# Sliding-window attention with one packed block of weights: the scores of the block behind go where the mask would be

## The chip, the cores and the metric

The kernel runs on one core of a Trainium2 chip, as one launch. The metric is the device time of that launch in microseconds. Engines in the text: PE is TensorE, DVE is VectorE, ACT is ScalarE, POOL is GpSimd, SP is SyncE, which here only issues DMAs.

## What is computed

The input is x of 2 sequences, 4096 tokens, 256 channels, in fp32. First a recurrent block (a token mix, three projections, a scan over time, a group norm and an output projection) is added to a layer norm of x. Then, after another layer norm, two layers follow, each with local attention and a gated feed-forward part, and a residual around all. The attention is what matters here:

```
WINDOW = 128, HEADS = 8, DIM_HEAD = 64, DEPTH = 2
bq = q.reshape(b, h, w, WINDOW, d) * 8
bk, bv = look_around(k), look_around(v)      # the block behind, and the own block: 256 keys
sim = einsum('bhwid,bhwjd->bhwij', bq, bk)
mask = (i < j) | (i > j + WINDOW) | (j == -1)
attn = softmax(where(mask, -max, sim))
out = einsum('bhwij,bhwjd->bhwid', attn, bv)
```

So query i of a block sees the keys i to 127 of the block behind, and the keys 0 to i of its own: 129 keys of the 256, whatever i is. The first block of a sequence has none behind it and sees only its own.

## The kernel before

The work is noted down in program order by functions that each issue a few operations (`project`, `scores`, `softmax`, `transpose_p`, `values`, `output` and so on). A planner (`Plan`) takes them all, with the dependences it finds from overlapping regions of tiles, and simulates five engines and eight PSUM banks with a table of costs (`cost`). At every step it gives an engine the operation that can start first, ties going to the smaller row (about the window's number). That order is then written out, and is fixed on the chip: each engine and the SP queue go through their own list, and an operation at the head of a list that waits holds all behind it. Operations noted with `either` (copies out of PSUM, and the products `scaled`) go to VectorE or ScalarE, whichever the planner has free first. Matmuls noted within one `piece` stay together. Since the planner emits all operations from one function, most rows of the profile have one line, L497, and are told apart by their tiles. `scaled` is L491 on DVE and L493 on ACT.

The planner charges a DMA 2000 ns and 512 bytes for every element of its largest operand's free size at 170 bytes a nanosecond, whatever the number of partitions, and lets such transfers follow one another.

There are 128 windows of attention: two sequences, two layers, 32 blocks of 128 tokens. Window n is worked on in one turn of a loop, while the projections of n+1 and the output and feed-forward of earlier ones are done. The recurrence of the first sequence runs ahead of all windows; that of the second runs beside the first 54 windows.

In one window:

- `project(n, j)` makes q, k and v, 128x512 each. v goes to a tile `vt` (three buffers). q and k are rotated on POOL and DVE, and `transpose_qk` turns them into `qT` and into one of the two slots of `kT`, by the parity of n.
- `scores(n)` is one piece: first `values(n - 1)`, then eight score products of 256 keys. They fill four banks (`sims`), each for two heads.
- `softmax(n, g)` takes bank g: for each of two heads one fused operation on DVE reads the bank, negates it, adds the mask, writes the tile `pr` in SBUF, and takes the minimum; ACT makes the exponential in place with its sum; a reciprocal; and `scaled` normalises. A bank is free once the fused operations have read it.
- `transpose_p(n, g)` turns the weights of two heads on TensorE, 128x128 at a time (four transposes into one bank), and copies them out as `pT`, 128x512.
- `values(n)` multiplies: for each head, `vt` of the window behind by its part of `pT`, and `vt` of the own window by the other part, both into one bank. It waits for the four `pT` of the window.

A window without one behind it does half of that. Four are of that kind.

Of the kernel before, what the change touches and what calls it, by code (L numbers as in the profile page):

```python
# [10 lines left out]
AF = mybir.ActivationFunctionType  # L11
ALU = mybir.AluOpType
AX = mybir.AxisListType
PSUM = bass.MemoryType.PSUM

P = 128
B, S, D = 2, 4096, 256
HD_A = 16
L, HEADS, DH, W = 2, 8, 64, 128
INNER = HEADS * DH  # L20
# [5 lines left out]
T = 512  # L26
NW = T // P
NB = S // T
# [4 lines left out]
MASKED = -3e38  # L33
# [12 lines left out]
)  # L46
WNOW = 3 * (2 * T + 2)
RA = 10764
PRS, PTS = 6, 4

# [22 lines left out]
class View:  # L75
# [51 lines left out]
    def to_broadcast(self, shape):  # L127
        return View(
            self.place,
            self.rows,  # L130
            np.broadcast_to(self.idx, shape[1:]),
            [*self.chain, ("to_broadcast", (shape,), {})],
        )

    def mask(self):
        n = self.place.size
# [34 lines left out]
class Plan:  # L171
# [35 lines left out]
    def bank(self, shape):  # L207

        return self.view(Place(T, True), 0, shape)
# [9 lines left out]
    @contextmanager  # L219
    def piece(self):  # L220

        self.open = []
        yield
        self.open = None
# [276 lines left out]
def kernel(ctx: ExitStack, tc: tile.TileContext, a: dict, out: bass.AP):  # L501
# [6 lines left out]
    tile_of, bank, piece = plan.tile, plan.bank, plan.piece  # L508
    act, dve, either = nc.scalar.copy, nc.vector.tensor_copy, nc.either.copy
# [4 lines left out]
    ident, gmat = (mats[:, i, :] for i in range(2))  # L514
# [286 lines left out]

    mask = tile_of([P, 3 * W], "mask")
    lnp = tile_of([P, L, 2, 2], "lnp")
    b1 = tile_of([P, L, 2, NM], "b1")
    qks = tile_of([P, L, 4 * DH], "qks")

    def later_loads():
        nc.sync.dma_start(out=wot, in_=a["w_ot"])  # L810
        nc.sync.dma_start(out=mask[:, : 2 * W], in_=a["c_mask"])
        nc.sync.dma_start(out=mask[:, 2 * W :], in_=a["c_mask"][:, :W])
        nc.sync.dma_start(out=lnp, in_=a["p_ln"])
        nc.sync.dma_start(out=b1, in_=a["p_b1"])
        nc.sync.dma_start(out=qks, in_=a["p_qk"].partition_broadcast(P))
# [16 lines left out]
            nc.sync.dma_start(out=w2, in_=a["w_2"][l])  # L832


    kT = tile_of([P, HEADS // 2, 2, W], "kT")


    hm = tile_of([P, NM, T], "hm")
# [4 lines left out]
    G_LAST = 5  # L843
    blocks = [(l, b, c) for b in range(B) for l in range(L) for c in range(NB)]
    xs, xTs, hs, x1s, zs, hTs, rems = ({} for _ in range(7))
    tabs, qks_of, vts, qTs, pos, sims, prs, sqs, t2s = ({} for _ in range(9))


    def load(k):
# [73 lines left out]
    def project(n, j):  # L923
        k, w = divmod(n, NW)
        xT = xTs[k]

        hT = (xT[:, 0, 1 + w * P : 1 + (w + 1) * P], xT[:, 1, w * P : (w + 1) * P])
        pm = bank([P, INNER])
        for i in range(2):
            nc.tensor.matmul(  # L930
                pm, hT[i], wqkv[:, i, j * INNER : (j + 1) * INNER], start=(i == 0), stop=(i == 1)
            )
        if j == 2:
            vts[n] = tile_of([P, INNER], "vt", 3)
            either(vts[n], pm)
            return
        if j == 0:
            qks_of[n] = tile_of([P, 2, HEADS, DH], "qk", 2)
        either(qks_of[n][:, j].rearrange("p h d -> p (h d)"), pm)

    def square(n):
        qk = qks_of[n]
# [42 lines left out]
    def transpose_qk(n):  # L985
        qk = qks_of.pop(n)
        qT = qTs[n] = tile_of([P, HEADS // 2, P], "qT", 2)
        for j, dst in ((1, kT[:, :, n % 2, :]), (0, qT)):
            pt = bank([P, HEADS // 2, P])
            for hp in range(HEADS // 2):  # L990
                nc.tensor.transpose(
                    pt[:, hp, :],
                    qk[:, j, 2 * hp : 2 * hp + 2, :].rearrange("p h d -> p (h d)"),
                    ident,
                )
            either(dst, pt)

    def seen(n):

        me = n % 2  # L1000
        if n % (NB * NW) == 0:
            return slice(me, me + 1), mask[:, W : 2 * W], ((me, n),)
        if me:
            return slice(0, 2), mask[:, : 2 * W], ((0, n - 1), (1, n))
        return slice(0, 2), mask[:, W:], ((0, n), (1, n - 1))

    def scores(n):


        cs, _, _ = seen(n)  # L1010
        qT = qTs[n]
        sims[n] = [bank([P, 2, 2, W]) for _ in range(4)]
        with piece():
            if n:
                values(n - 1)
            for hp in range(HEADS // 2):
                for r in range(2):
                    s, m = divmod(hp, 2)
                    nc.tensor.matmul(
                        sims[n][2 * s + r][:, m, cs, :].rearrange("p c j -> p (c j)"),  # L1020
                        qT[r * DH : (r + 1) * DH, hp, :],
                        kT[r * DH : (r + 1) * DH, hp, cs, :].rearrange("p c j -> p (c j)"),
                        start=True,
                        stop=True,
                    )

    def softmax(n, g):

        cs, msk, _ = seen(n)
        sim = sims[n][g]  # L1030
        pr = prs[n, g] = tile_of([P, 2, 2, W], "pr", PRS)
        nmx = tile_of([P, 2], "nmx", 8)
        sums = tile_of([P, 2], "sums", 8)
        for m in range(2):
            ph = pr[:, m, cs, :].rearrange("p c j -> p (c j)")

            nc.vector.tensor_tensor_reduce(
                ph,
                sim[:, m, cs, :].rearrange("p c j -> p (c j)"),
                msk,  # L1040
                -1.0,
                3.0e38,
                ALU.add,
                ALU.min,
                nmx[:, m : m + 1],
            )
            nc.scalar.activation(
                ph, ph, AF.Exp, bias=nmx[:, m : m + 1], scale=-1.0, accum_out=sums[:, m : m + 1]
            )
        nc.vector.reciprocal(sums, sums)  # L1050
        for m in range(2):
            ph = pr[:, m, cs, :].rearrange("p c j -> p (c j)")
            nc.either.scaled(ph, ph, sums[:, m : m + 1])

    def transpose_p(n, g):

        cs, _, srcs = seen(n)
        pr = prs.pop((n, g))
        ppt = bank([P, 2, 2, W])
        for m in range(2):  # L1060
            for c, _ in srcs:
                nc.tensor.transpose(ppt[:, m, c, :], pr[:, m, c, :], ident)
        pT = prs[n, g, "T"] = tile_of([P, 2, 2, W], "pT", PTS)
        either(pT[:, :, cs, :], ppt[:, :, cs, :])

    def values(n):

        _, _, srcs = seen(n)
        po = bank([P, HEADS // 2, P])
        pTs = [prs.pop((n, g, "T")) for g in range(4)]  # L1070
        for hp in range(HEADS // 2):
            s, m = divmod(hp, 2)
            for i, (c, src) in enumerate(srcs):
                for r in range(2):
                    h = 2 * hp + r
                    nc.tensor.matmul(
                        po[r * DH : (r + 1) * DH, hp, :],
                        vts[src][:, h * DH : (h + 1) * DH],
                        pTs[2 * s + r][:, m, c, :],
                        start=(i == 0),  # L1080
                        stop=(i == len(srcs) - 1),
                    )
        pos[n] = po

# [202 lines left out]
    for j in range(3):  # L1287
        project(0, j)
# [6 lines left out]
    for n in range(NN + 6):  # L1295
        k, w = divmod(n, NW)
        here, ahead, behind = n < NN, n + 1 < NN, 0 < n <= NN
        plan.at(n)
        if here:
            transpose_qk(n)  # L1300
# [22 lines left out]
            rotate(n + 1, 0)  # L1323
        if here:
            scores(n)
        elif n == NN:
            with piece():
                values(n - 1)
# [23 lines left out]
        fill(n, 0)  # L1352
        if here:
            transpose_p(n, 0)
            transpose_p(n, 1)
        if ahead:
            project(n + 1, 2)
            cosines(n + 1)
        fill(n, 1)
        if here:  # L1360
            transpose_p(n, 2)
            transpose_p(n, 3)
        if ahead:
            rotated(n + 1)
        fill(n, 2)
# [7 lines left out]
def _constants():  # L1373

    f = np.float32
    p = np.arange(P)
    mats = np.zeros((P, 2, P), f)
    mats[:, 0, :] = np.eye(P)
    mats[:, 1, :] = (p[:, None] // HD_A == p[None, :] // HD_A) / f(HD_A)
    j = np.arange(2 * W)  # L1380
    mask = np.where((j[None, :] >= p[:, None]) & (j[None, :] <= p[:, None] + W), f(0), f(MASKED))

    half = np.arange(0, DH, 2, dtype=f)
    inv = f(1) / np.power(f(10000.0), half / f(DH))
    t = np.arange(S, dtype=f)
    freqs = t[:, None] * inv[None, :]
    base = (half + f(0.4 * DH)) / f(1.4 * DH)
    power = (t - f(S // 2)) / f(W // 2)
    scale = np.power(base[None, :], power[:, None])
    cos, sin = np.cos(freqs), np.sin(freqs)  # L1390
    rot = np.empty((S, 2, 2, DH), f)
    for q, sc in ((0, scale * f(8)), (1, f(1) / scale)):
        rot[:, 0, q, :] = np.concatenate([cos * sc, cos * sc], -1)
        rot[:, 1, q, :] = np.concatenate([-sin * sc, sin * sc], -1)
    rot = rot.reshape(NB * NW, P, 4 * DH)
    return {"c_mats": mats, "c_mask": mask.astype(f), "c_rot": np.ascontiguousarray(rot)}
# [52 lines left out]
```

## Time and profile before

| | |
|---|---|
| median of 3 runs | 3110.5 us (3108.18 to 3110.82) |
| the profiled execution, its own time | 3112.78 us |
| its span, first to last instruction | 3110.8 us |
| granted TensorE clock, mean | 0.995 |
| PE, DVE, ACT, POOL busy | 98%, 82%, 60%, 43% |
| transposes of attention weights | 2016, 270.5 us busy |
| mean rate of the DMA engines | 42 GB/s |

A row of the profile's groups reads: line, engine, operation, output<-inputs, shapes, count | busy us, mean ns of one | us of idle time of that engine just before them, and what ended it. The busy time of a group of matmuls includes the tail of the last one, since they are pipelined; the distance from one start to the next is what an instruction takes from the engine. In the timeline a row is: start, duration, engine, operation, and in brackets how long the engine had been idle and what released it.

### The profile page before, as it was taken

What the parts mean: (1) busy time and instruction counts of PE and PEld (TensorE: products, weight loads), DVE (VectorE), ACT (ScalarE), POOL (GpSimd) and SP (SyncE); (2) the same over time, 40 slices, a digit from 0 to 9 for tenths busy, and PEclk for the clock granted to TensorE, in tenths of its full rate; (3) what the DMA queues carried; (4) which work ended last, traced back from release to release, by engine and by line L of the source; (5) the groups of instructions that cost most, each with busy time, mean ns of one, the idle gap of its engine ahead of it and who ended that gap; (6) DMA issues with size and microseconds to landing.
All of it is one profiled execution on the core that took longest, in us unless ns stands there. A gap on an engine that the chain in (4) does not pass through costs nothing.

```text
span 3110.8 us, 47943 instructions
## 1 busy us (share of the span) xinstructions
PE 3061.6 (98%) x16368; PEld 2030.8 (65%) x16368; DVE 2539.1 (82%) x6306; ACT 1865.0 (60%) x4401; POOL 1339.6 (43%) x1581
## 2 busy tenths in 40 slices
PE   8979999999999999999999999999999999999998
PEld 3456666666666666666666666666666666666665
DVE  7889988888888888887787878787877777877774
ACT  6877866666666766665554555554555555555552
POOL 2227534443444444444444444443433444444440
PEclk9989999999999999999999999999999999999999
DMA  3222001110111210111112110111101110111000
GB/s 101 80 75 70 31 30 45 45 38 30 43 48 45 67 31 26 34 37 31 35 47 73 50 46 26 38 41 38 35 25 54 45 36 30 33 33 33 28 22 19
DMA packets 114837, 131.82 MB, mean 42 GB/s; under 512 B 13344, under 2 KB 100128, under 8 KB 114080
## 3 DMA queue, kind: packets, MB, share of 16 engines
q1 hardware_dynamic: 114592, 128.75, 13.2%
q8 instruction: 129, 2.11, 0.3%
q14 instruction: 116, 0.95, 0.1%
HBM read 78.38 MB, written 33.55 MB: 36 GB/s over the span
## 4 chain that ended last, share of the span: by engine, by line
PE 80%; DVE 10%; ACT 4%; POOL 2%; issue 2%; DMA 2%; SPq 0%; POOLq 0%; DVEq 0%; ACTq 0%
PE bank L497 80%; DVE arena L497 3%; ACT arena L497 1%; DMA h<-x 1%; DVE pr L497 1%; DVE sq L497 1%; DVE qk L497 1%; POOL rs L497 1%; ACT L497 1%; DVE hm L497 1%; POOL rn L497 1%; DVE x L497 1%; ACT qk L497 0%; SPq L497 0%; DVE pT L497 0%
## 5 line engine op out<-in xcount | busy, mean ns | idle before, releaser
L497 ACT ACTIVATE pr<-pr,nmx 128x256 f32<-128x256 f32 (+1 forms) x1024 | 504.2, 493 | 388.8 <-DVE nmx L497 388.4
L497 PE MATMUL bank<-wqkv,xT 128*128 128x512 f32 x1536 | 731.6, 599 | 0.0
L497 POOL TENSOR_TENSOR t<-qk,tab 128x256 f32<-128x256 f32 x512 | 387.6, 777 | 727.9 <-DVE qk L497 420.3
L497 PE MATMUL bank<-hT,w 128*128 128x512 f32 (+1 forms) x1408 | 645.9, 594 | 0.0
L497 PEld LDWEIGHTS bank<-hT,w 128*128 128x128 f32 (+1 forms) x1408 | 253.7, 189 | 251.9 <-issue 242.1
L497 PEld LDWEIGHTS bank<-wqkv,xT 128*128 128x128 f32 x1536 | 264.7, 190 | 229.9 <-issue 224.9
L497 DVE CUSTOM_DVE_ANT_0 pr<-bank,mask 128x256 f32<-128x256 f32 (+1 forms) x1024 | 372.5, 413 | 36.1 <-PE bank L497 36.0
L497 POOL TENSOR_TENSOR rn<-rn,mhalf 128x16 f32<-128x16 f32 x128 | 380.9, 2976 | 10.3
L497 PE MATMUL bank<-w,hm 128*128 128x256 f32 x1536 | 352.1, 379 | 0.0
L497 PEld LDWEIGHTS bank<-w,hm 128*128 128x128 f32 x1536 | 289.2, 190 | 57.7 <-issue 21.9
L497 PEld LDWEIGHTS bank<-mats,pr 128*128 128x128 f32 x2016 | 237.1, 141 | 114.2 <-issue 78.8
L493 ACT ACTIVATE pr<-pr,sums 128x256 f32<-128x256 f32 (+1 forms) x610 | 284.7, 495 | 35.1 <-DVE sums L497 33.4
L497 PEld LDWEIGHTS bank<-pT,vt 128*64 128x64 f32 x4032 | 217.5, 137 | 95.9 <-issue 88.3
L497 PE MATMUL bank<-mats,pr 128*128 128x128 f32 x2016 | 270.5, 273 | 2.3 <-DVE pr L491 1.2
L497 PE MATMUL bank<-kT,qT 64*128 64x256 f32 (+1 forms) x2048 | 253.4, 386 | 4.1 <-DVE nmx L497 4.1
L497 PE MATMUL bank<-pT,vt 128*64 128x128 f32 x4032 | 248.4, 276 | 0.0
L497 PE MATMUL bank<-wo,oT 128*128 128x256 f32 x1024 | 244.8, 382 | 2.2 <-ACT oT L497 1.2
L497 PEld LDWEIGHTS bank<-wo,oT 128*128 128x128 f32 x1024 | 192.2, 190 | 79.0 <-issue 38.3
L497 ACT COPY pT<-bank 128x512 f32<-128x512 f32 (+1 forms) x275 | 150.1, 572 | 120.0 <-PE bank L497 119.4
L497 PEld LDWEIGHTS bank<-kT,qT 64*128 64x128 f32 x2048 | 184.9, 186 | 44.6 <-issue 19.8
L497 POOL TENSOR_SCALAR rs<-mv 128x1 f32<-128x1 f32 x192 | 98.4, 517 | 248.4 <-DVE mv L497 242.2
L497 PE MATMUL bank<-arena,wold 128*128 128x256 f32 (+1 forms) x600 | 193.1, 447 | 0.0
(139 smaller groups left out, 4988.1 us busy)
## 6 DMA issues: line engine op xcount, KB each, us to landing
tab<-in_c_rot_dram SPq DMA_DIRECT2D x128, 128.0 KB
z<-zd SPq DMA_DIRECT2D x16, 512.0 KB
x<-in_x_dram SPq DMA_DIRECT2D x16, 512.0 KB
x1d<-x SPq DMA_DIRECT2D x16, 512.0 KB
x<-x1d SPq DMA_DIRECT2D x16, 512.0 KB
h<-x SPq DMA_DIRECT2D x128, 64.0 KB
xmd<-x SPq DMA_DIRECT2D x64, 128.0 KB
x<-xmd SPq DMA_DIRECT2D x16, 512.0 KB
```

Source lines behind the costliest of these rows:

```text
L493: self.nc.scalar.activation(dst, src, AF.Copy, scale=scale)
L497: getattr(getattr(self.nc, o.eng), name)(*args, **kw)
```

## The change

The 256 scores of a query are packed to 129. Where the causal mask would strike out a score of the own block (key j after query i), the score of key j-1 of the block behind is put in, which is one that the query sees. The oldest distance, key 127 of the block behind, is seen by all queries, and keeps a column of its own in front. The layout of a score bank becomes "behind, then own" for all windows, so `kT` gets a third slot; every second window a DMA copies the last slot to the first.

- On DVE, a predicated copy in PSUM (with the mask `packs`) puts the scores over the masked ones, and a reduction takes the minimum of the 129. The minus sign moves into the rotation table. ACT's exponential reads the bank itself and writes the 129 weights to `pr`, now one tile for eight heads, two buffers.
- `transpose_p` is called twice, with four heads of one block of 128 columns each. The turned weights are copied out as `pT`, and DVE also multiplies them by the mask `backs`, which keeps only those that belong to the block behind: `pB`. In the second call the first columns of the eight heads are turned together (128x8), copied to `last`, and a DMA puts them into row 0 of `pB`.
- `values` multiplies `pT` by the own values, and `pB` by `dv`, the difference between the value behind and the own value in whose place its weight sits. `differences(n)` makes `dv`: two DMAs shift the values behind by one row, POOL subtracts, and a DMA puts the value of key 127 in row 0.
- `vt` has two buffers for three, `pT` two for four, `pB`, `vr` and `dv` one.

```diff
-PRS, PTS = 6, 4
+PRS, PTS, PBS = 2, 2, 1
...
-        nc.sync.dma_start(out=mask[:, : 2 * W], in_=a["c_mask"])
-        nc.sync.dma_start(out=mask[:, 2 * W :], in_=a["c_mask"][:, :W])
+        for i, t in enumerate((packs, backs, later)):
+            nc.sync.dma_start(out=t, in_=a["c_mask"][:, i, :])
...
-    kT = tile_of([P, HEADS // 2, 2, W], "kT")
+    kT = tile_of([P, HEADS // 2, 3, W], "kT")
...
-            vts[n] = tile_of([P, INNER], "vt", 3)
+        vts[n] = tile_of([P, INNER], "vt", 2)
...
+    def differences(n):
+        if lone(n):
+            return
+        old, v = vts[n - 1], vts[n]
+        vr = tile_of([P, INNER], "vr")
+        dv = dvs[n] = tile_of([P, INNER], "dv")
+        nc.sync.dma_start(out=vr[1:P, :], in_=old[: P - 1, :])
+        nc.sync.dma_start(out=vr[0:1, :], in_=old[P - 1 : P, :])
+        nc.gpsimd.tensor_tensor(dv, vr, v, ALU.subtract)
+        nc.sync.dma_start(out=dv[0:1, :], in_=old[P - 1 : P, :])
...
+        if me == 2:
+            nc.sync.dma_start(out=kT[:, :, 0, :], in_=kT[:, :, 2, :])
...
     def softmax(n, g):
...
-            nc.vector.tensor_tensor_reduce(ph, sim..., msk, -1.0, 3.0e38, ALU.add, ALU.min, nmx[:, m : m + 1])
-            nc.scalar.activation(
-                ph, ph, AF.Exp, bias=nmx[:, m : m + 1], scale=-1.0, accum_out=sums[:, m : m + 1]
-            )
+            nc.vector.copy_predicated(
+                sim[:, :, W + 1 :],
+                packs[:, : W - 1].bitcast(mybir.dt.int32).unsqueeze(1).to_broadcast([P, 2, W - 1]),
+                sim[:, :, : W - 1],
+            )
+            nc.vector.tensor_reduce(nmx, sim[:, :, W - 1 :], AX.X, ALU.min)
...
+            nc.scalar.activation(
+                prs[n][:, h0 + 2 * m, off:], sim[:, m, W - 1 + off :], AF.Exp,
+                bias=nmx[:, m : m + 1], scale=-1.0, accum_out=sums[:, m : m + 1],
+            )
...
-    def transpose_p(n, g):
+    def transpose_p(n, s):
...
+        for h in range(4):
+            nc.tensor.transpose(ppt[:, h, :], pr[:, 4 * s + h, 1:], ident)
+        pT = pTs[n, s] = tile_of([P, 4, W], "pT", PTS)
+        either(pT, ppt)
...
+        nc.vector.tensor_tensor(
+            pBs[n][:, 4 * s : 4 * s + 4, :], ppt, backs.unsqueeze(1).to_broadcast([P, 4, W]), ALU.mult,
+        )
+        if s:
+            pt = bank([P, W])
+            nc.tensor.transpose(pt[:HEADS, :], pr[:, :, 0], ident)
+            last = tile_of([P, W], "last", 2)[:HEADS]
+            either(last, pt[:HEADS, :])
+            nc.sync.dma_start(out=pBs[n][0:1], in_=last)
...
     def values(n):
...
+                    w = (dvs if i else vts)[n]
+                    p = pBs[n][:, h, :] if i else own[h // 4][:, h % 4, :]
...
             scores(n)
+            differences(n)
...
-            transpose_p(n, 1)
...
-            transpose_p(n, 2)
-            transpose_p(n, 3)
+            transpose_p(n, 1)
...
-    for q, sc in ((0, scale * f(8)), (1, f(1) / scale)):
+    for q, sc in ((0, scale * f(-8)), (1, f(1) / scale)):
```

More of the change, by code (lines that the diff above doesn't have):

```diff
@@ L133, in to_broadcast, with bitcast @@
         )
+    def bitcast(self, dtype):
+        return View(self.place, self.rows, self.idx, [*self.chain, ("bitcast", (dtype,), {})])
     def mask(self):
@@ L793, in group_norm @@
             nc.vector.tensor_tensor(of, bet, of, ALU.subtract)
-    mask = tile_of([P, 3 * W], "mask")
+    packs, backs, later = (tile_of([P, W], t) for t in ("packs", "backs", "later"))
     lnp = tile_of([P, L, 2, 2], "lnp")
@@ L845 @@
     xs, xTs, hs, x1s, zs, hTs, rems = ({} for _ in range(7))
-    tabs, qks_of, vts, qTs, pos, sims, prs, sqs, t2s = ({} for _ in range(9))
+    tabs, qks_of, vts, qTs, pos, sims, prs, pTs, pBs, dvs, sqs, t2s = ({} for _ in range(12))
     def load(k):
@@ L932, in project @@
             )
-        if j == 2:
-            vts[n] = tile_of([P, INNER], "vt", 3)
-            either(vts[n], pm)
+        if j < 2:
+            if j == 0:
+                qks_of[n] = tile_of([P, 2, HEADS, DH], "qk", 2)
+            either(qks_of[n][:, j].rearrange("p h d -> p (h d)"), pm)
             return
-        if j == 0:
-            qks_of[n] = tile_of([P, 2, HEADS, DH], "qk", 2)
-        either(qks_of[n][:, j].rearrange("p h d -> p (h d)"), pm)
+        vts[n] = tile_of([P, INNER], "vt", 2)
+        either(vts[n], pm)
+    def differences(n):
[8 more added lines that the diff above has]
+        nc.sync.dma_start(out=dv[0:1, :], in_=old[P - 1 : P, :])
     def square(n):
@@ L987, in transpose_qk @@
         qT = qTs[n] = tile_of([P, HEADS // 2, P], "qT", 2)
-        for j, dst in ((1, kT[:, :, n % 2, :]), (0, qT)):
+        me = 1 + n % 2
+        for j, dst in ((1, kT[:, :, me, :]), (0, qT)):
             pt = bank([P, HEADS // 2, P])
@@ L996, in transpose_qk, with lone @@
             either(dst, pt)
[L998 to L1005, printed above, removed]
+        if me == 2:
+            nc.sync.dma_start(out=kT[:, :, 0, :], in_=kT[:, :, 2, :])
+    def lone(n):
+        return n % (NB * NW) == 0
     def scores(n):
-        cs, _, _ = seen(n)
         qT = qTs[n]
-        sims[n] = [bank([P, 2, 2, W]) for _ in range(4)]
+        me = 1 + n % 2
+        cs = slice(1, 2) if lone(n) else slice(0, 2)
+        ks = slice(me, me + 1) if lone(n) else slice(me - 1, me + 1)
+        sims[n] = [bank([P, 2, 2 * W]) for _ in range(4)]
         with piece():
@@ L1019, in scores @@
                     nc.tensor.matmul(
-                        sims[n][2 * s + r][:, m, cs, :].rearrange("p c j -> p (c j)"),
+                        sims[n][2 * s + r][:, m, cs.start * W : cs.stop * W],
                         qT[r * DH : (r + 1) * DH, hp, :],
-                        kT[r * DH : (r + 1) * DH, hp, cs, :].rearrange("p c j -> p (c j)"),
+                        kT[r * DH : (r + 1) * DH, hp, ks, :].rearrange("p c j -> p (c j)"),
                         start=True,
@@ L1027, in softmax @@
     def softmax(n, g):
-        cs, msk, _ = seen(n)
         sim = sims[n][g]
-        pr = prs[n, g] = tile_of([P, 2, 2, W], "pr", PRS)
+        if g == 0:
+            prs[n] = tile_of([P, HEADS, 1 + W], "pr", PRS)
+        h0 = g // 2 * 4 + g % 2
         nmx = tile_of([P, 2], "nmx", 8)
         sums = tile_of([P, 2], "sums", 8)
-        for m in range(2):
[L1035 to L1045, printed above, removed]
-            )
-            nc.scalar.activation(
-                ph, ph, AF.Exp, bias=nmx[:, m : m + 1], scale=-1.0, accum_out=sums[:, m : m + 1]
+        if lone(n):
+            for m in range(2):
+                nc.vector.tensor_tensor_reduce(
+                    sim[:, m, W:],
+                    sim[:, m, W:],
+                    later,
+                    1.0,
+                    3.0e38,
+                    ALU.add,
+                    ALU.min,
+                    nmx[:, m : m + 1],
+                )
+        else:
+            nc.vector.copy_predicated(
[4 more added lines that the diff above has]
+            nc.vector.tensor_reduce(nmx, sim[:, :, W - 1 :], AX.X, ALU.min)
+        off = 1 if lone(n) else 0
+        for m in range(2):
+            nc.scalar.activation(
+                prs[n][:, h0 + 2 * m, off:],
+                sim[:, m, W - 1 + off :],
+                AF.Exp,
+                bias=nmx[:, m : m + 1],
+                scale=-1.0,
+                accum_out=sums[:, m : m + 1],
             )
@@ L1051, in softmax @@
         for m in range(2):
-            ph = pr[:, m, cs, :].rearrange("p c j -> p (c j)")
+            ph = prs[n][:, h0 + 2 * m, off:]
             nc.either.scaled(ph, ph, sums[:, m : m + 1])
-    def transpose_p(n, g):
[L1057 to L1064, printed above, removed]
+    def transpose_p(n, s):
+        pr = prs[n]
+        ppt = bank([P, 4, W])
+        for h in range(4):
+            nc.tensor.transpose(ppt[:, h, :], pr[:, 4 * s + h, 1:], ident)
+        pT = pTs[n, s] = tile_of([P, 4, W], "pT", PTS)
+        either(pT, ppt)
+        if lone(n):
+            return
+        if s == 0:
+            pBs[n] = tile_of([P, HEADS, W], "pB", PBS)
+        nc.vector.tensor_tensor(
+            pBs[n][:, 4 * s : 4 * s + 4, :],
+            ppt,
+            backs.unsqueeze(1).to_broadcast([P, 4, W]),
+            ALU.mult,
+        )
[5 more added lines that the diff above has]
+            nc.sync.dma_start(out=pBs[n][0:1], in_=last)
@@ L1066, in values @@
     def values(n):
-        _, _, srcs = seen(n)
         po = bank([P, HEADS // 2, P])
-        pTs = [prs.pop((n, g, "T")) for g in range(4)]
+        own = [pTs.pop((n, s)) for s in range(2)]
         for hp in range(HEADS // 2):
-            s, m = divmod(hp, 2)
-            for i, (c, src) in enumerate(srcs):
+            for i in range(1 if lone(n) else 2):
                 for r in range(2):
                     h = 2 * hp + r
+                    w = (dvs if i else vts)[n]
+                    p = pBs[n][:, h, :] if i else own[h // 4][:, h % 4, :]
@@ L1076, in values @@
                     nc.tensor.matmul(
                         po[r * DH : (r + 1) * DH, hp, :],
-                        vts[src][:, h * DH : (h + 1) * DH],
-                        pTs[2 * s + r][:, m, c, :],
+                        w[:, h * DH : (h + 1) * DH],
+                        p,
                         start=(i == 0),
-                        stop=(i == len(srcs) - 1),
+                        stop=(i == 1 or lone(n)),
                     )
@@ L1379, in _constants @@
     mats[:, 1, :] = (p[:, None] // HD_A == p[None, :] // HD_A) / f(HD_A)
-    j = np.arange(2 * W)
-    mask = np.where((j[None, :] >= p[:, None]) & (j[None, :] <= p[:, None] + W), f(0), f(MASKED))
+    packs, backs = p[None, :] >= p[:, None], p[None, :] < p[:, None]
+    mask = np.stack([packs, backs, np.where(packs & ~np.eye(P, dtype=bool), -MASKED, 0)], 1)
     half = np.arange(0, DH, 2, dtype=f)
```

## The prediction, made before the changed kernel was built

> **What bounds the kernel now.** I read first the page's busy table and the chain that ended last, then the busy time by stage, then the groups with shapes kept apart, and last the timeline of one attention window.
>
> The page:
>
> ```profile
> span 3110.8 us, 47943 instructions
> ...
> PE 3061.6 (98%) x16368; PEld 2030.8 (65%) x16368; DVE 2539.1 (82%) x6306; ACT 1865.0 (60%) x4401; POOL 1339.6 (43%) x1581
> ...
> PE 80%; DVE 10%; ACT 4%; POOL 2%; issue 2%; DMA 2%; SPq 0%; POOLq 0%; DVEq 0%; ACTq 0%
> ```
>
> Busy time by stage, one row from the half in which the second batch's recurrence runs beside the windows and one from the half behind it (columns: PE, PEld, DVE, ACT, POOL busy, granted clock, DMA share, GB/s):
>
> ```profile
> 700.00:900.00 200.00, 199.51 (x1116) 136.41 (x1115) 176.01 (x435) 130.44 (x302) 84.67 (x104) 1.00 0.12 36
> ...
> 1700.00:1900.00 200.00, 200.00 (x1103) 134.69 (x1102) 161.29 (x413) 105.45 (x266) 85.74 (x103) 1.00 0.17 52
> ```
>
> TensorE has no idle time from 1500 us nearly to the end, at the full granted clock; VectorE is at 81% there and at 88% earlier. So a microsecond of TensorE work is a microsecond of time, as long as the other engines keep up. Groups by shape:
>
> ```profile
> L497 PE MATMUL bank<-mats,pr 128*128 128x128 f32 x2016 | 270.5, 273 | 2.3 <-DVE pr L491 1.2 <-ACT pr L493 0.8
> ...
> L497 ACT ACTIVATE pr<-pr,nmx 128x256 f32<-128x256 f32 x992 | 491.8, 497 | 381.2 <-DVE nmx L497 380.9
> ...
> L497 DVE CUSTOM_DVE_ANT_0 pr<-bank,mask 128x256 f32<-128x256 f32 x992 | 364.9, 417 | 35.9 <-PE bank L497 35.9
> L493 ACT ACTIVATE pr<-pr,sums 128x256 f32<-128x256 f32 x593 | 278.6, 498 | 35.0 <-DVE sums L497 33.4
> ...
> L491 DVE TENSOR_SCALAR pr<-pr,sums 128x256 f32<-128x256 f32 x399 | 170.1, 439 | 3.0
> ...
> L497 DVE COPY pT<-bank 128x512 f32<-128x512 f32 x234 | 155.2, 675 | 0.6 <-PE bank L497 0.5
> L497 DVE TENSOR_REDUCE rn<-sq 128x16 f32<-128x1024 f32 x128 | 155.1, 1212 | 18.2 <-ACT sq L497 17.7
> ...
> L497 DVE TENSOR_TENSOR x<-x,bank 128x512 f32<-128x512 f32 x32 | 21.8, 681 | 16.7 <-PE bank L497 16.7
> ...
> L497 ACT ACTIVATE pr<-pr,nmx 128x128 f32<-128x128 f32 x32 | 12.4, 389 | 7.6 <-DVE nmx L497 7.6
> ```
>
> 2016 transposes of the weights are 124 windows of 16, and 4 windows without a window behind (first of a layer and batch) of 8. From the timeline, the parts of two neighbouring windows:
>
> ```profile
> 2009.40 0.60 PE L497 MATMUL bank<-mats,pr 128*128 128x128 f32 x4
> ...
> 2009.84 1.88 PE L497 MATMUL bank<-hT,w 128*128 128x512 f32 x4
> ...
> 2014.25 1.97 PE L497 MATMUL bank<-pT,vt 128*64 128x128 f32 x32
> ...
> 2019.72 0.42 DVE L497 CUSTOM_DVE_ANT_0 pr<-bank,mask 128x256 f32<-128x256 f32 x1
> ...
> 2023.34 1.04 PE L497 MATMUL bank<-mats,pr 128*128 128x128 f32 x8
> ...
> 2024.21 1.88 PE L497 MATMUL bank<-wqkv,xT 128*128 128x512 f32 x4
> ...
> 2024.39 0.49 ACT L497 ACTIVATE pr<-pr,nmx 128x256 f32<-128x256 f32 x1
> ...
> 2027.03 0.33 SPq L497 DMA_DIRECT2D tab<-in_c_rot_dram  x1
> ...
> 2029.17 1.50 POOL L497 TENSOR_TENSOR tab<-tab,qks 128x256 f32<-128x256 f32 x1 [1.94 <-DMA tab<-in_c_rot_dram]
> ```
>
> Eight transposes start at 2023.34 and the next matmul at 2024.21: 0.87 us, so 0.108 us each (four from 2009.40 to 2009.84 say 0.11). The 273 ns of the group is the latency of one; only the 0.108 counts.
>
> One rule speaks against reading TensorE as the bound. The Trainium skill (Perfetto Trace Analysis, "Identifying the Most-Contended Engine") says that matmul occupancy is no measure of headroom, and to judge by weight-load occupancy, 65% here; VectorE's 82% would then be the limit, and the extra VectorE work below (+0.65 us in each of 124 windows) would cost 81 us. The row weighs more: matmuls start a pitch apart with 0.0 idle before them, for 1500 us. I go by the row.
>
> **The change, part by part, for one of the 124 windows.**
>
> *TensorE.* 16 transposes become 8, and one more (128x8) turns the column of the oldest key: 7 x 0.108 = 0.756 us less. The value product stays at 16 matmuls (its second half has another weight and another moving tile of the same size), scores stay too. 124 x 0.756 = 93.7 us. The four lone windows keep their 8.
>
> *Mask and maximum on VectorE.* Eight fused mask-and-minimum operations go, 0.345 us apart in the timeline of that window (duration 0.417): 2.76 us. In come four predicated copies of 254 elements, in place in PSUM, and four minimum reductions of 258. The trace has no predicated copy and nothing that VectorE writes into PSUM. Lower bound: the fused operation's pitch, 0.345; upper: the slowest elementwise kind in the trace, a scan of 256, 0.74 to 0.80. The nearest row is an addition over one bank (681 ns for 512), which with the 414 ns of its 256 form gives 0.41; the reduction, from 1212 ns for 1024, is about the same. Does the second overlap the first? The fused ones do (0.345 of 0.417). The skill (VectorE: DVE Perf Modes, "The DRAIN you can't avoid") says the next operation waits until the pipeline is empty and advises fewer operations; with that, 8 x 0.41 = 3.28. By the row's pitch alone, 2.76. Each reduction needs its copy, but the next copy doesn't need that reduction, so I take one of each: 4 x (0.415 + 0.345) = 3.04, +0.28. Upper with the scan's price: +1.4 more.
>
> *Other VectorE work.* Two multiplications of a bank by a mask, 0.64 each by the 681 ns row less overlap: +1.28. Transposed weights are copied out twice, not four times; VectorE had 47% of them, so 0.94 copies of 0.61 go: -0.57. Normalising is on 129 and not 256: VectorE had 40% of eight, 3.2 x (0.43 - 0.28) = -0.48. The copy of the turned column: +0.14 (half of 0.28). Net +0.65 us; with the dear predicated copy +2.1.
>
> *ScalarE.* Eight exponentials at 0.389 for 0.497 (-0.86; they now read PSUM, and bank copies of 512 on ScalarE, 0.58, are no dearer than 0.62 from SBUF), 4.8 normalisations at 0.1 less (-0.5), one copy less (-0.6): about -1.9 us. Nothing on the path: it is at 53 to 65%.
>
> *POOL.* One subtraction of 512. Its 256-element kinds take 0.78 to 1.16 us, so 1.5 to 2.3; 43% busy becomes some 50%. It waits for the shifted values (DMA) and the values of the window before; behind it wait the next window's rotations, which have some 10 us before their transposes. While it runs, VectorE operations with two SBUF inputs may be held: bound 0 to 1.5 us, taken 0.2, covered where VectorE has slack.
>
> *SP and DMA.* Per window two DMAs for the shifted values, one for row 0 of the differences, one for row 0 of the products, and every second window one that moves the last keys to the slot in front: 4.5 more, at 0.33 to 0.65 us of issue (table and shift DMAs), about 2.3 us on a queue that mostly waits for producers. Bytes grow by about 0.4 MB a window, at a DMA share of 0.1 to 0.17. The differences are made ten microseconds ahead and cost nothing while that lead holds.
>
> *The new wait.* Row 0 of the products goes transpose, copy, DMA, and only then may values(n), and in the same piece scores(n+1), start; everything behind them on TensorE waits too, and so does the softmax. The cover is what TensorE does between the last weight transpose and the values: 4.24 us in the window shown (2010.00 to 2014.25), and 5.1, 6.0 and 8.5 to 10.3 in the others of each group of four. A table DMA needs 2.14 us (2027.03 to 2029.17), a lone shift DMA about 3.1 to 3.7; with 0.4 to 1.2 for the copy and its place in the queue, 2.6 to 4.9 us. So at worst 0.7 us in one window of four: 124/4 x 0.7 = 21 us; taken 5. Without the cover it would be all of it, 3.5 us a window.
>
> *Banks.* A score bank used to be free after its fused operations (the last ends at 2020.1 here); now it is held until its exponentials (2024.9): two banks of eight some 4.5 us longer. The turned weights need two banks fewer. Taken at nothing net while three or four banks are left for projections that drain in about 3 us each; the rival below prices it.
>
> *Sum.* -93.7 of TensorE. Given back: row 0, +5; in the 52 windows beside the recurrence, where VectorE goes from 88% to about 94% and TensorE already loses 0.25 to 1.4%, +0.3 us each, +16. About -72 us. Against the profiled execution (span 3110.8, 3112.8 with what lies around it) that is 3041; it was 2.3 us above the median of the runs, so 3039 against 3110.5.
>
> **The rivals.**
>
> 1. VectorE becomes the bound beside the recurrence. There a window takes some 23 us and VectorE 20.4 of them; with the dear predicated copy, 22.5, which is all of the shortened 22.4. Then that half gains nothing and the other half 72 x 0.756 = 54 us less a little: about 3062. For it: 88% already, and one operation of unknown price. Against it: copies may move to ScalarE, which gains 1.9 us a window.
>
> 2. Slower: score banks. If TensorE finds no bank while the last two wait for exponentials, it loses a projection's time, 1.72 us (four matmul instructions of 0.43). That outweighs the saving once it happens in over 54 of 124 windows (93.7 / 1.72). In every window: +213 - 94, about 3230. For it: exponentials run to 8 or 9 us after the scores, in the stretch with most projections. Against it: ScalarE's load falls, so they come earlier, and the planner counts banks when it writes the order.
>
> 3. The row 0 chain takes more than the 4.24/5.1/6.0 us of cover. Break-even is at 6.1 us ((6.1 - 4.24) + (6.1 - 5.1) + (6.1 - 6.0) over 4 is 0.75); at 5.6 it gives back half, 3070. The planner charges this DMA over 5 us, more than a DMA showed, so it may also reorder everything around it: a change that only reorders would land near 3110.
>
> **How the numbers follow.** Main case, 0.60: 3015 to 3060, at 3039. Part of it eaten by VectorE or the chain, 0.14: 3060 to 3104. No change, within 0.2% (6 us, about what can be told from no change), 0.05. Slower by banks, chain or order, 0.21: 3117 to 3230. The range 3012 to 3130 leaves out about 0.03 below and 0.15 above. Faster 0.74, same 0.05, slower 0.21.
>
> **What would show it.** Weight transposes 1148 for 2016, still 0.108 us apart; TensorE still without idle behind 1500 us, and window groups of four of about 82 us where they were 85 to 87; predicated copies near 0.41 us; VectorE at 84 to 87% behind 1500 us and 93 to 95% before; no TensorE wait on the row DMA above 10 us in total. Wrong, if TensorE's weight loads wait on that DMA or on ScalarE's reading of score banks, if the predicated copy is over 0.7 us, or if TensorE drops under 97% behind 1500 us.

## The result, and the profile after

The changed kernel took 4024.4 us (4022.9 to 4026.2) against 3110.7: 1.294 times as long, 95% interval 1.2918 to 1.2962. The forecast was 3039. The experiments below show that the packing itself gains about what was forecast of it; what failed is one of the new transfers.

The page of the changed kernel, the parts shown before:

```profile
span 4022.0 us, 47294 instructions
...
PE 3224.9 (80%) x15500; PEld 2075.3 (52%) x15500; DVE 2479.5 (62%) x5234; ACT 1722.5 (43%) x4597; POOL 1429.8 (36%) x1705
...
PE 30%; DVE 24%; SPq 21%; DMA 13%; ACT 6%; issue 4%; POOL 4%; DVEq 0%; POOLq 0%; ACTq 0%
PE bank L500 30%; SPq L500 21%; DMA h<-x 10%; DVE qk L500 3%; DVE arena L500 3%; DVE bank L500 3%; DVE nmx L500 2%; DVE sq L500 2%; DVE rn L500 2%; ACT arena L500 1%; DVE x L500 1%; POOL rn L500 1%; POOL rs L500 1%; DMA pB<-last 1%; DVE pr L494 1%
```

No engine is near full. The chain has a member that was 0% before, SP's queue, and next to it the transfer h<-x, the shift by one token that `shift(n)` makes for the feed-forward part. Nothing in the diff touches it. VectorE's waits say the same (waiting engine and tile, what it waited for, us in all, times, longest):

```profile
DVE st L500 <- DMA h<-x: 934.8, 115, 12.3
```

Before, this wait was 84.9 us. The rise of 850 us is of the size of the whole loss (914 us). One window in the timeline of the changed kernel:

```profile
2506.01 0.66 SPq L500 DMA_DIRECT2D vr<-vt  x1
...
2508.54 11.44 SPq L500 DMA_DIRECT2D h<-x  x3
...
2523.38 0.43 DVE L500 BATCH_NORM_STATS2 st<-h 128x6 f32<-128x256 f32 x1 [9.55 <-DMA h<-x]
2523.85 0.18 DVE L500 BATCH_NORM_AGGREGATE mv<-st 128x2 f32<-128x6 f32 x1
2523.95 1.19 DVE L500 TENSOR_TENSOR qk<-sq,rn 128x1024 f32<-128x1024 f32 x1
...
2525.28 1.94 PE L500 MATMUL bank<-mats,qk 128*128 128x128 f32 x8 [5.43 <-DVE qk L500]
```

The three DMAs of h, issued in some 2.2 us before, hold SP for 11.44 us. VectorE stands at the statistics of h for 9.55 us, and behind them in its list are the rotated q and k, for which TensorE then waits 5.43 us. The eight transposes after that take 1.94 us, not 1.04: TensorE's granted clock is 0.50 from 2525 to 2528 us, where it was 1.00 from 2510 to 2518 (mean 0.902 over the run, 0.995 before).

What ran meanwhile is seen in the DMA view of this stretch, 2510 to 2518 us (packets and bytes; then the queue's packets, MB, and the time of its packets as a share of 16 engines):

```profile
DMA packets 98, 0.20 MB, mean 25 GB/s; under 512 B 0, under 2 KB 0, under 8 KB 98
...
q1 hardware_dynamic: 98, 0.20, 6.6%
```

98 packets of 2 KB, one after the other, 82 ns each: that is vr<-vt, 127 rows of 2 KB, and 6.6% of sixteen engines is about one engine. All 127 rows take 127 x 82 ns = 10.4 us. The shift of h has 127 rows as well. The same view of the kernel before, 2022.9 to 2024.9 us, had it in plain sight:

```profile
DMA packets 56, 0.03 MB, mean 14 GB/s; under 512 B 0, under 2 KB 56, under 8 KB 56
...
q1 hardware_dynamic: 56, 0.03, 4.9%
```

There too 512 bytes at a time went, in the slices of the view in which they moved, at some 20 GB/s, and 4.9% of sixteen engines is less than one: some 3 us for 63.5 KB. The Trainium skill (DMA: Bandwidth & Descriptors, "Why a DMA increments its semaphore by 16 and not by 1") gives the reason, and these rows agree: a transfer is spread over the largest number of engines up to 16 that divides its rows, so 127 rows, a prime, go to one.

The theory then: the new 127-row copy takes that one engine for 10 us just ahead of the shift of h, which needs the same engine. Rivals: (B) the new order of all queues, which the planner wrote with dear DMAs; (C) the score banks held for ScalarE, or the chain of row 0.

### The profile page after: what moved, and what is told of

Read it like the earlier page. It is cut to its first block, busy times and chain, and to the rows that moved or that the text cites. A ratio compares the mean times of both kernels' runs of the same rounds, so it can differ in the third digit from the quotient of the medians.

```text
span 4022.0 us, 47294 instructions
## 1 busy us (share of the span) xinstructions
PE 3224.9 (80%) x15500; PEld 2075.3 (52%) x15500; DVE 2479.5 (62%) x5234; ACT 1722.5 (43%) x4597; POOL 1429.8 (36%) x1705
## 4 chain that ended last, share of the span: by engine, by line
PE 30%; DVE 24%; SPq 21%; DMA 13%; ACT 6%; issue 4%; POOL 4%; DVEq 0%; POOLq 0%; ACTq 0%
PE bank L500 30%; SPq L500 21%; DMA h<-x 10%; DVE qk L500 3%; DVE arena L500 3%; DVE bank L500 3%; DVE nmx L500 2%; DVE sq L500 2%; DVE rn L500 2%; ACT arena L500 1%; DVE x L500 1%; POOL rn L500 1%; POOL rs L500 1%; DMA pB<-last 1%; DVE pr L494 1%
## 5 line engine op out<-in xcount | busy, mean ns | idle before, releaser
L500 PE MATMUL bank<-wqkv,xT 128*128 128x512 f32 x1536 | 791.1, 647 | 0.0
L500 DVE BATCH_NORM_STATS2 st<-h 128x6 f32<-128x256 f32 x128 | 54.6, 426 | 961.2 <-DMA h<-x 934.8
L500 ACT ACTIVATE pr<-bank,nmx 128x129 f32<-128x129 f32 (+1 forms) x1024 | 361.4, 364 | 351.8 <-DVE nmx L500 351.4
L500 PE MATMUL bank<-mats,qk 128*128 128x128 f32 x1024 | 171.4, 319 | 277.9 <-DVE qk L500 277.7
L500 PE MATMUL bank<-pB,dv 128*64 128x128 f32 x1984 | 229.1, 309 | 164.4 <-issue 89.3
L500 PEld LDWEIGHTS bank<-mats,qk 128*128 128x128 f32 x1024 | 144.3, 166 | 327.5 <-DVE qk L500 199.0
L496 ACT ACTIVATE pr<-pr,sums 128x129 f32<-128x129 f32 (+1 forms) x739 | 260.7, 400 | 95.3 <-DVE sums L500 93.4
L500 ACT ACTIVATE sq<-qk 128x1024 f32<-128x1024 f32 x128 | 135.1, 1055 | 356.3 <-DVE qk L500 355.9
L500 POOL TENSOR_TENSOR tab<-tab,qks 128x256 f32<-128x256 f32 x128 | 111.6, 873 | 401.4 <-DMA tab<-in_c_rot_dram 335.3
L500 PE MATMUL bank<-mats,pr 128*128 128x128 f32 x1148 | 186.0, 283 | 79.7 <-ACT pr L496 50.4
L500 PEld LDWEIGHTS bank<-mats,pr 128*128 128x128 f32 x1148 | 136.2, 138 | 211.5 <-ACT pr L496 96.9
```

Of the source, the lines that this page charges most:

```text
L496: self.nc.scalar.activation(dst, src, AF.Copy, scale=scale)
L500: getattr(getattr(self.nc, o.eng), name)(*args, **kw)
```

## Experiments

**The copy in two parts.** The list of operations keeps its order; only at the moment of issue the 127 rows become 112 and 15.

```diff
             name = o.name
+            if name == "dma_start" and isinstance(o.kw["out"], View) and o.kw["out"].shape[0] == P - 1:
+                to, of = o.kw["out"], o.kw["in_"]
+                if to.idx.size in (512,):          # e2: (512, 128)
+                    for r in (slice(0, 112), slice(112, P - 1)):
+                        self.nc.sync.dma_start(out=get(to[r]), in_=get(of[r]))
+                    continue
```

> The changed kernel with its order of instructions left as it is; only the copy of 127 rows of values by 2 KB (vr) is issued as two copies, of 112 and of 15 rows. Theory A: a copy of 127 rows is carried by one DMA engine alone (25 GB/s, 10.3 us for 254 KB), the 127-row shift of h behind it waits for that engine and holds the SP queue for about 10 us, and VectorE, POOL and then TensorE stand behind h. Then the split takes nearly all of the loss away: 3040 to 3120 us, the issue of h back to about 0.7 us each, VectorE waiting under 150 us on h. Rival B: the new order of the queues (written by the planner with dear DMAs) is what costs; the order is the same here and SP has one DMA more, so 3900 to 4050. Rival C: score banks held, or the chain of row 0: over 3500.

Measured: 3077.7 us (3075.6 to 3080.3), 0.9894 of the kernel before (0.9877 to 0.991). The same bytes in the same order with one DMA more, and 947 us are gone. VectorE's wait for h is 92.8 us in place of 934.8, and three DMAs of h are mostly issued in 2.3 us again. B and C, which put it over 3500, fall.

> As e1_split_vr, and the 127-row shift of h (63.5 KB) is issued as 112 and 15 rows as well. Theory A: h lands about 2 us earlier than in e1_split_vr, worth 0 to 60 us against it: 3000 to 3100. Rivals B and C: no different from their figure for e1_split_vr.

Measured: 3037.7 us (3035.0 to 3039.6), ratio 0.9765 (0.975 to 0.9779): another 40 us. Page of this kernel, and its VectorE wait:

```profile
span 3035.9 us, 47682 instructions
...
PE 2972.1 (98%) x15500; PEld 1935.5 (64%) x15500; DVE 2476.0 (82%) x5234; ACT 1723.4 (57%) x4597; POOL 1441.7 (47%) x1705
...
PE 81%; DVE 10%; ACT 4%; POOL 2%; issue 1%; DMA 1%; SPq 0%; DVEq 0%; POOLq 0%; ACTq 0%
...
DVE st L506 <- DMA h<-x: 26.6, 32, 3.5
```

The shape of the page before is back, with 89 us less of TensorE. Against the changed kernel's page the loss shows two parts: for the same 15500 matmuls TensorE was busy 3224.9 us there and 2972.1 here, at mean granted clocks of 0.902 and 0.993. So about a quarter of the 986 us between the two spans is TensorE working more slowly, and the rest is TensorE idle.

**126 and 1.** As the first, with `(slice(0, 126), slice(126, P - 1))`.

> As e1_split_vr, but the 127 rows of values go as 126 and 1: 126 is 14 times 9, 127 is prime. If the number of engines is the largest up to 16 that divides the rows, 126 rows need 9 packets in turn (0.74 us at 82 ns each) and the time is that of e1_split_vr: 3070 to 3090. If a transfer must have a multiple of 16 rows to be spread, or if its size alone counts, it stays over 3900.

Measured: 3078.0 us in one run, the time of 112 and 15. One row less in the large part makes the whole difference; 126 is no multiple of 16, but 14 divides it. The DMA view, here over 2022.6 to 2023.6 us, shows the copy of the values spread over the engines, at ten times the rate of the whole one (25 GB/s, 6.6%):

```profile
DMA packets 143, 0.24 MB, mean 245 GB/s; under 512 B 24, under 2 KB 24, under 8 KB 143
...
q1 hardware_dynamic: 143, 0.24, 73.7%
```

**Another queue.** The 127 rows whole, issued by ScalarE.

```diff
...
+                if o.kw["out"].idx.size == 512:
+                    self.nc.scalar.dma_start(out=get(o.kw["out"]), in_=get(o.kw["in_"]))
+                    continue
```

> The changed kernel with the copy of 127 rows of values whole, but issued from ScalarE's DMA queue; the shift of h stays on SP. If SP's queue in order is what holds h, it is free now, and 3080 to 3200 are left. If it is the one DMA engine that both use, h still shares it: its packets may take turns with the other queue's, so h comes in 6 to 7 us instead of 13, 3250 to 3700. ScalarE's own issue of some 0.6 us a window is covered.

Measured: 3944.1 us in one run, 2% under the changed kernel and above both of my ranges. The two rows of its timeline that matter (the first from ScalarE's queue):

```profile
2516.43 0.63 ACTq L492 DMA_DIRECT2D vr<-vt  x1
...
2519.03 8.47 SPq L504 DMA_DIRECT2D h<-x  x3
```

The copy is on ScalarE's queue and the shift of h still holds SP for 8.5 us; VectorE waits 918.3 us for h in all. The DMA view from 2518.5 to 2526 us has both queues (q10 is ScalarE's):

```profile
DMA packets 96, 0.16 MB, mean 21 GB/s; under 512 B 0, under 2 KB 26, under 8 KB 96
...
q10 hardware_dynamic: 70, 0.14, 5.8%
q1 hardware_dynamic: 26, 0.01, 0.6%
```

Rows of the values (2 KB) and rows of h (512 bytes) move in the same stretch, and the two queues together come to 6.4% of sixteen engines, about one engine. So the order of SP's queue is not what makes h late; the engine that both transfers use is. I had expected h in 6 to 7 us: in this window VectorE started on it 14.8 us after SP began to issue it (2519.03 to 2533.80), as in the changed kernel (2508.54 to 2523.38). Why the issue holds SP although the copy is on another queue stays open.

**The suspected cost alone, in the kernel before.** Copies of 127 rows by 1664 bytes to an unused tile `spare`, whole or as 112 and 15.

```diff
+            if name == "dma_start" and isinstance(o.kw["out"], View) and o.kw["out"].shape[0] == P - 1:
+                for r in (slice(0, P - 1),):       # e5: (slice(0, 112), slice(112, P - 1))
+                    self.nc.sync.dma_start(
+                        out=get(self.spare[1:P, :][r]), in_=get(self.constant[: P - 1, :][r])
+                    )
```

> The kernel before in its own order, with one more DMA just ahead of each 127-row shift of h: 127 rows of 1664 bytes (206 KB) from a constant tile to a tile that nobody reads. Theory A: one DMA engine is taken for some 8.4 us in every window and h comes that much later, with about 2 us of slack: 128 times 5 to 8 us, so 3700 to 4100. Rival B (order, not the copy): 3110 to 3160.

Measured: 3311.6 us in one run, +201. The sign is right and the size far under my range:

```profile
2004.15 0.66 SPq L489 DMA_DIRECT2D spare<-qks  x1
...
2014.13 3.17 SPq L502 DMA_DIRECT2D h<-x  x3
```

This copy waits for nothing, so SP issues it as soon as it comes to it, here 10 us ahead, and then waits for x. Much of its 8 us lies in that time.

> The same added bytes as e4_before_copy127, but as 112 and 15 rows. Theory A: 16 engines share it, under 1 us; h comes 0.5 to 1.5 us later for the issue of two more DMAs: 3110 to 3200. If the bytes or the number of DMAs on SP were what costs, it would be as slow as e4_before_copy127.

Measured: 3111.6 us in one run, the time of the kernel before. Bytes and the number of DMAs on SP cost nothing here.

To give the copies no head start, I made them read what the shift reads: three copies of `o.kw["in_"]` into `spare`, ahead of each shift.

> The kernel before in its own order, with three more copies of the 127-row shift (63.5 KB each, to a tile that nobody reads) ahead of each real one. They wait for the same data as the real one, so they can't run early as the copy of e4_before_copy127 did (it was issued 6 to 17 us ahead of the shift). One DMA engine is then busy some 8 to 9 us before h's rows: if lateness of h alone makes the loss, 128 times 5 to 8 us, so 3700 to 4150. If only the late values (vr) do: 3110 to 3300.

Measured: 4271.9 us in one run, +1161, 9.1 us a window (a little over my range).

```profile
PE 3344.8 (78%) x16368; PEld 2185.1 (51%) x16368; DVE 2545.1 (60%) x6306; ACT 1869.0 (44%) x4401; POOL 1298.9 (30%) x1581
...
DVE st L502 <- DMA h<-x: 1145.8, 127, 15.0
```

With 256 scores, no packing, no `dv`, the kernel before becomes slow in the same way when the rows of h come late. So a late shift of h is enough; the values need not be late for it. In each of the slow kernels SP is held while h is late, so how much of the loss comes from h itself and how much from what SP issues behind it, such as the rotation tables, is not separated by these runs.

**What the packing is worth.** The kernel before with its own shift of h split, order unchanged:

> The kernel before, in its own order, with its 127-row shift of h issued as 112 and 15 rows. Theory A (one DMA engine carries 127 rows, about 3 us for 63.5 KB): h lands some 2 us earlier; the chain that ended last gave 1.3% (40 us) to these DMAs, nearly all in the half beside the recurrence: 3070 to 3105. If it gains as much as the same edit gained on the changed kernel (40 us), the packed scores are worth the difference of the two with good shifts, 33 us; if it gains nothing, 72.

Measured: 3103.8 us (3103.0 to 3105.4), ratio 0.9977 (0.9968 to 0.9986): 7 us, at the slow end of my range. Both with good shifts, the packing gains 3103.8 - 3037.7 = 66 us.

**The wait for row 0.** The second kernel above, with the DMA pB<-last left out at issue.

> As e2_split_both, without the DMA that puts the oldest key's weights into row 0 of the products: row 0 keeps its masked value, so the oldest key's part is left out. The prediction put the wait for it at 5 us in all (bound 21). Theory: 3028 to 3040 against 3037.7. Rival, that the row 0 chain is what keeps the packed kernel from more: under 3010.

Measured: 3039.6 us (3038.0 to 3040.9), ratio 0.9771 (0.9755 to 0.9787), no different from 3037.7. The new wait on the path of `values` costs nothing that can be measured.

**A plan that knows.** Both shifts split in the plan, and the planner's price of a DMA by rows:

```diff
+            rows = views[0].shape[0]
+            engines = 16 if rows == 1 else max(k for k in range(1, 17) if rows % k == 0)
+            o.passes = 4 * rows * max(v.idx.size for v in views) / (25 * engines)
+            o.step, o.time = 500, 2000 + o.passes
```

> The changed kernel with both 127-row shifts split in the plan itself, and the planner's price of a DMA by rows: bytes over 25 GB/s times the engines (the largest count up to 16 that divides the rows; 16 for one row), 500 ns of issue. A new order of all queues follows. Theory: the order was not what cost, so 3000 to 3045, within 1.5% of e2_split_both. Rival, that the planner's dear DMAs gave a poor order: under 3000.

Measured: 3022.5 us (3021.6 to 3022.9), ratio 0.9714 (0.97 to 0.9729). It beats both kernels, and the new order is worth 15 us over the 3037.7 of the kernel with both shifts split.

> The kernel before with its 127-row shift split in the plan and the planner's DMA price by rows, as in e9_planned: what the same planning gives without the packed scores. The packed kernel gained 15 us by it. Expected 3080 to 3105, so that the packed scores are worth 60 to 85 us of the 3022.5 of e9_planned; if it comes down to 3060 or less, the planning and not the packing made most of e9_planned's gain.

Measured: 3106.9 us (3104.4 to 3108.8), ratio 0.9986 (0.9979 to 0.9993). This is just above my range: the same planning does nothing for the kernel before beyond its split shift. So of the 88 us that the best version gains, 84 stand between the two with the same planning.

## Why the prediction was wrong, point by point

*The step that failed* is "SP and DMA", and with it the sentence that "the differences are made ten microseconds ahead and cost nothing while that lead holds". I sized the copies by their bytes at a mean DMA share of 0.1 to 0.17, and by SP's issue. The term should have been 127 rows x 82 ns on one engine, 10.4 us a window. I also asked only who waits for the new copy (POOL, early enough), and not what else needs the engine that it takes: the shift of h, which has the same 127 rows and stands in front of q and k in VectorE's list. I had even quoted the symptom: a lone shift of 63.5 KB needing 3.1 to 3.7 us where a table of 128 KB needs 2.14. I took it for a spread of latency and did not ask why half the bytes took longer.

*The bound* was read rightly. With good shifts TensorE is at 98% again, and busy 1399.6 of the 1400 us from 1500 to 2900; its lower work is the gain.

*TensorE's term*, 0.756 us in each of 124 windows, held. Window starts are 85.5 us apart in fours in the planned version where the kernel before had 88.5 in the same stretch (1700 to 2000 us), so 3.0 for four; near the end four take 82.0 to 82.1 where they took 85.1. The weight transposes number 1024 and 124:

```profile
L506 PE MATMUL bank<-mats,pr 128*128 128x128 f32 x1024 | 158.0, 274 | 5.6 <-ACT pr L502 2.6 <-DVE pr L500 2.4
...
L506 PE MATMUL bank<-mats,pr 128*8 128x128 f32 x124 | 33.8, 273 | 0.0
```

*VectorE's term* had the wrong sign: its busy time fell from 2539 to 2476 us, where I had added 0.65 us a window, 81 us in all. The groups of the kernel with both shifts split:

```profile
L506 DVE TENSOR_REDUCE nmx<-bank 128x2 f32<-128x258 f32 x496 | 191.5, 415 | 0.0
L506 DVE COPY_PREDICATED bank<-packs,bank 128x254 f32<-128x254 int32 x496 | 186.0, 420 | 24.2 <-PE bank L506 24.0
L506 DVE TENSOR_TENSOR pB<-bank,backs 128x512 f32<-128x512 f32 x248 | 169.5, 683 | 52.0 <-ACT pT L506 51.7
...
L500 DVE TENSOR_SCALAR pr<-pr,sums 128x129 f32<-128x129 f32 x271 | 81.5, 329 | 2.2
...
L506 DVE COPY pT<-bank 128x512 f32<-128x512 f32 x100 | 68.0, 680 | 2.7 <-PE bank L506 1.5
...
L506 DVE COPY last<-bank 8x128 f32<-8x128 f32 x23 | 6.2, 269 | 0.0
```

The durations of the main operations are those that I took (0.42 and 0.41, 0.68). What differs:

- The copies of two banks follow each other and then the two reductions (four in 1.34 us, from 2504.93 to 2506.27 in the changed kernel's timeline), 0.335 us a start. That makes 2.68 us for the eight, where I had 3.04. The emptying of the pipeline, which I had weighed in for half, does not show between these operations; the section that I cited for it also says that an operation which is not held starts earlier, and I had passed over that.
- The planner gave VectorE 271 normalisations of 992 instead of 40%, and 100 copies of `pT` instead of 47%. For a narrow tile its price of a normalisation is 220 ns on ScalarE and 288 on VectorE, which I could have worked out from `cost`.

An estimate from these rows and those before, against 81 us: -10 for mask and minimum (0.08 us less in each of 124 windows), -89 for normalising, -87 for `pT`, +170 for `pB` and +6 for `last`, so -10 us. Beyond that, VectorE's copies out of banks to other tiles fell from 421 to 364 us in all, since the planner gave more of them to ScalarE; I had no term for that.

*Given back.* I had 5 us for row 0 and 16 beside the recurrence. Row 0: nothing. From the first window's scores to the 55th's, the kernel with both shifts split takes 1194 us where the kernel before took 1207; from there to the last, 1520 for 1576. So the first part, where I forecast 23 us of gain, gave 13, and some 5 of these are the split's: the kernel before with its own shift split takes 1202. The second part gave 56, where I had 54. In the planned version the first part gives 26.

*The rivals.* VectorE as the bound: no, it is busy 175.8 of the 200 us from 700 to 900 in the kernel with both shifts split, 88% as before, and not 93 to 95%. Score banks: no, since TensorE has next to no idle time there behind 1500 us. The row 0 chain: no, since leaving its DMA out gains nothing. (Its price in the prediction was also too low: a chain of 5.6 us would by the same sum have given back 58 of the 94 us, not half.) None of them held the mechanism. That the sum of 3039 meets the 3037.7 of the repaired kernel is partly luck, since a split of the old shift is in it as well; the packing alone, 66 us by one comparison and 84 by the other, stands around the 72 forecast.

## What to carry to other kernels

Before a transfer is added, count the engines that will carry it, not its bytes alone: in these runs 127 rows went to one engine at 25 GB/s, and 126 + 1 or 112 + 15 cured it. Shifting a tile of 128 rows by one partition makes this row count, so split it. Then ask what else uses that engine and which engine's list stands behind that: here a transfer whose own result was made ten microseconds ahead cost 947 us through another one that had little to spare.

## What the runs showed of the hardware that I had not expected

- While the one engine was busy, the issue of the next DMAs to it held SP: 11.44 us for three, against mostly 2.2 to 2.3 before. It was so too when the copy was on ScalarE's queue (8.47 us). The runs do not show why.
- Packets of 2 KB on one engine followed each other every 82 ns, 25 GB/s; the same copy as 126 rows and 1 went at 245 GB/s.
- A predicated copy in place in PSUM, 254 elements, takes 420 ns, and in runs of two copies and two reductions one starts every 335 ns, like the fused operations that they replaced (345).
